# The weight products of a graph layer from three float32r passes over 12-bit parts, with the accumulator kept in DRAM

## The chip, the cores and the metric

The kernel runs on one core of a Trainium2 chip. Times are device microseconds of that core, smaller is better. Abbreviations as in the profile: PE is TensorE (matmuls), PEld its weight loads, DVE is VectorE, ACT is ScalarE, POOL is GpSimd, SP issues DMA transfers. SBUF is the memory on the chip, PSUM holds what the matmuls sum, DRAM is the memory beside it.

## What is computed

Two layers of a graph network on 1250 rows of 1024 columns with 40000 edges, then a mixture of experts, each with a layer normalization ahead of it and added to its input:

```
def _sage_layer(h, edge_src, edge_dst, deg_inv, W_self, W_neigh, b):
    msg = h[edge_src]
    agg = jax.ops.segment_sum(msg, edge_dst, num_segments=h.shape[0])
    mean = agg * deg_inv[:, None]
    return h @ W_self + mean @ W_neigh + b
h   = relu(_sage_layer(layernorm(x), ..., W_self0, W_neigh0, b0))
x   = x + _sage_layer(h, ..., W_self1, W_neigh1, b1)
t   = layernorm(x)
out = x + t + moe(t)       # router rw1, rw2; two of eight experts per row
```

All inputs are fp32. This case is about the second `_sage_layer`: two products of 1250 x 1024 by 1024 x 1024, and one sum over the edges.

## The kernel before

**Stages.** `gnn_windows` turns the edges into a matrix `C` of counts (1250 x 1250) in SBUF while PE does the first layer. The first layer leaves its result transposed in `hT1` (128 partitions, 8 slices k of the 1024 columns, 1250 rows each). Then comes the second layer, and `moe` after it. Rows are worked in 10 blocks of 128 (the last has 98), output columns in two halves of 512.

**Second layer, in order.**
1. `y_half` (L682): y = h times one half of `W_neigh1`, written as two float32r tiles, `zh` (y rounded by ACT) and `zl` (the rest), by `split` (L388).
2. `sum_half` (L697): for each block, 20 float32r matmuls of `C` with `zh` and `zl` (L708), scaled by 1 / degree (`dinv_p`), added to x + b1 (L704 on POOL, L712 on DVE), and stored to `v_d` in DRAM. Both are done for each half.
3. `own_half` (L740): the same kind of product with the two halves of `W_self1`, added to `xa`, a tile of all 10 blocks by 1024 columns that was read back from `v_d` (L734). In the second half each finished block goes to `finish` (L767): `after_layers` (L344) normalizes it (bn_stats L328 and L330, scale L335 on DVE), adds the normalized row (L349 on POOL) and writes both to DRAM, and `turn_back` (L777) transposes it on PE (L784) and copies it with ACT (L788) to `hT1` for the router.

**The products** are plain fp32, by a scheme of seven quarter products instead of eight for a pair of blocks j and 4 + j: `two_blocks` (L630) multiplies the blocks or their sums `T1` to `T4` with the weight quarters or their sums `S1` to `S4` (`weight_sums`, L590; 256 columns a product, L638). DVE makes the sums before a half begins. Blocks 8 and 9 are multiplied directly (`plain_rows`, L621, matmuls L625).

**Memory.** One tile `L` (L91) holds `hT1`, then `SC` (four rows of 1024 columns for scratch and rows) and `WW` (a weight half of 16 KB per partition, which DMA fills: `load_half`, L129). `h0T`, the first layer's input, and later `ts` with the sums share one place (tag "a").

**What sets the order.** A scheduler orders the instructions of each engine before the kernel runs, from the order in the code and its own estimate of when operands are there; each engine then works through its list in that order. `keep_in_program_order` pins the weight loads. In the second layer nothing is ordered by hand. PSUM has rings of three banks `mm` (tile `ps`) and three `mmb` (tile `psb`). The router in `moe` starts with products that need no sums (L1173, L1128), then needs `token_sums` (L1154, DVE, tile `xw`), whose memory is that of the second layer's own tiles, so it waits until the last result row has gone to DRAM.

Of the kernel before, what the change touches and what calls it, by code (L numbers as in the profile page):

```python
# [28 lines left out]
def kernel(  # L29
# [61 lines left out]
    L = land.tile([P, NT + 4 * D + 2 * WQ], F32, name="L")  # L91
    hT1 = L[:, :NT].rearrange("p (k n) -> p k n", k=KD)
    SC = L[:, NT : NT + 4 * D]
    WW = L[:, NT + 4 * D :]

# [32 lines left out]

    def load_half(w, h, t=WW):  # L129

        t = t.rearrange("p (k n) -> p k n", k=KD)
        tc.keep_in_program_order(
            nc.sync.dma_start(
                out=t, in_=w[:, h * HALF : (h + 1) * HALF].rearrange("(k p) n -> p k n", p=P)
            )
        )
        return t
# [206 lines left out]
    def after_layers(b, xa, t):  # L344

        m = rows[b]
        layernorm(t, xa[:, b, :], m)
        nc.sync.dma_start(out=t_d[blk(b), :], in_=t[:m])
        nc.gpsimd.tensor_tensor(xa[:m, b, :], xa[:m, b, :], t[:m], ALU.add)  # L349
        nc.sync.dma_start(out=out[blk(b), :], in_=xa[:m, b, :])  # L350


    def gnn_windows():
# [20 lines left out]
        ones_r = cpool.tile([P, P], F32R, name="ones_r")  # L374
        nc.gpsimd.memset(ones_r.bitcast(F32), 1.0)
# [6 lines left out]
        yl = yp.tile([P, NB, QW], F32R, name="yl")  # L382
        win = yp.tile([P, NB * WIN], F16, name="win")
# [148 lines left out]
        for q in range(4):  # L532
# [8 lines left out]
            if q == 0:  # L541
# [4 lines left out]
                for c0, n in cchunks:  # L546
# [7 lines left out]
                    nc.vector.reciprocal(dinv[:, c0 : c0 + n], dinv[:, c0 : c0 + n])  # L554
            for c0, n in cchunks:
# [23 lines left out]
        NA, KB = 4, KD // 2  # L579
        TC = NA * P  # L580
        ts = apool.tile([P, NB * D], F32, name="ts", tag="a")
        T1, T2, T4 = (
            ts[:, i * KB * TC : (i + 1) * KB * TC].rearrange("p (k n) -> p k n", k=KB)
            for i in range(3)
        )
        B12 = hT1[:, :KB, TC : 2 * TC]
        B22 = hT1[:, KB:, TC : 2 * TC]
        S_first = ts[:, 3 * KB * TC : 3 * KB * TC + 4 * KB * QW]

        def weight_sums(w, s):  # L590
            A11, A12, A21, A22 = w[:, :KB, :QW], w[:, KB:, :QW], w[:, :KB, QW:], w[:, KB:, QW:]
            S1, S2, S3, S4 = (
                s[:, i * KB * QW : (i + 1) * KB * QW].rearrange("p (k n) -> p k n", k=KB)
                for i in range(4)
            )
            tt(S1, A21, A22, ALU.add)
            tt(S2, S1, A11, ALU.subtract)
            tt(S3, A11, A21, ALU.subtract)
            tt(S4, A12, S2, ALU.subtract)
            return A11, A12, A22, S1, S2, S3, S4  # L600

        ws = weight_sums(w_half, S_first)

        tt(T1, B12, hT1[:, :KB, :TC], ALU.subtract)
        for k in range(0, KB, 2):
            ks = slice(k, k + 2)
            tt(T2[:, ks, :], B22[:, ks, :], T1[:, ks, :], ALU.subtract)
            tt(T4[:, ks, :], hT1[:, KB + k : KB + k + 2, :TC], T2[:, ks, :], ALU.subtract)
            for i in (k, k + 1):
                tt(B12[:, i, :], B22[:, i, :], B12[:, i, :], ALU.subtract)  # L610
        T3 = B12

        dinv_p = small.tile([P, NB], F32, name="dinv_p")
        for b in range(NB):
            m = rows[b]
            d_t = tmp[:, b % 4, :P]
            nc.vector.tensor_tensor(d_t[:m, :m], dinv[:m, blk(b)], ident[:m, :m], ALU.mult)  # L617
            nc.vector.tensor_reduce(dinv_p[:m, b : b + 1], d_t[:m, :m], AX.X, ALU.add)
        nc.sync.dma_start(out=row_of(3), in_=bcast(b1, D))

        def plain_rows(w, b):  # L621
            m = rows[b]
            ps = mm.tile([P, 512], F32, name="ps")
            for k in range(KD):
                nc.tensor.matmul(  # L625
                    ps[:m], hT1[:, k, blk(b)], w[:, k, :], start=(k == 0), stop=(k == KD - 1)
                )
            return ps[:m]

        def two_blocks(ws, j, u, store):  # L630

            A11, A12, A22, S1, S2, S3, S4 = ws
            b, b2 = j, NA + j
            js = slice(j * P, (j + 1) * P)

            def product(ps, rows_of, w, first):
                for k in range(KB):
                    nc.tensor.matmul(  # L638
                        ps, rows_of(k), w[:, k, :], start=(first and k == 0),
                        stop=(k == KB - 1), skip_group_check=not first,  # L640
                    )

            u2, u3 = u[:, 0, :], u[:, 1, :]
            pa = mm.tile([P, 512], F32, name="ps")[:, :QW]
            product(pa, lambda k: hT1[:, k, blk(b)], A11, True)
            nc.scalar.copy(u2, pa)
            pb = mm.tile([P, 512], F32, name="ps")[:, :QW]
            product(pb, lambda k: T2[:, k, js], S2, True)
            tt(u2, u2, pb, ALU.add)
            product(pa, lambda k: hT1[:, KB + k, blk(b)], A12, False)  # L650
            store(b, 0, pa, None)
            pc = mmb.tile([P, 512], F32, name="psb")[:, :QW]
            product(pc, lambda k: T3[:, k, js], S3, True)
            tt(u3, u2, pc, ALU.add)
            pd = mmb.tile([P, 512], F32, name="psb")[:, :QW]
            product(pd, lambda k: T1[:, k, js], S1, True)
            store(b2, 1, pd, u3)
            product(pc, lambda k: T4[:, k, js], A22, False)
            store(b, 1, pc, u2)
            product(pd, lambda k: hT1[:, KB + k, blk(b2)], S4, False)  # L660
            store(b2, 0, pd, u2)

        def ring(v, n):
            v = v.rearrange("p (a n) -> p a n", n=QW)
            i = [0]

            def take():
                i[0] += 1
                return v[:, i[0] % n, :]

            return v, take

        us, _ = ring(SC[:, :1024], 4)
        _, spare = ring(SC[:, 1024:2048], 4)
        xs = SC[:, : 3 * D].rearrange("p (a n) -> p a n", n=HALF)
        b1_r = row_of(3)

        with tc.tile_pool(name="y1", bufs=1, side="right") as y1:
# [3 lines left out]
            def y_half(ws):  # L682
                for b in range(2 * NA, NB):
                    split(yh[: rows[b], b, :], yl[: rows[b], b, :], plain_rows(w_half, b))

                def store(b, c, ps, u):
                    if u is not None:
                        t = spare()
                        tt(t, u, ps, ALU.add)
                        ps = t  # L690
                    cs = slice(c * QW, (c + 1) * QW)
                    split(yh[:, b, cs], yl[:, b, cs], ps)
# [38 lines left out]
        for h, order in enumerate((alone + paired, paired + alone)):  # L731
# [3 lines left out]
            if h == 0:  # L735
                w_last = load_half(w_self1, 1, more[:, : 2 * WQ])
# [920 lines left out]
```

## Time and profile before

| What | us |
|---|---|
| Median of 3 runs | 1162.01 (1161.81 to 1162.07) |
| The profiled execution, its own time | 1160.5 |
| Its span from the first to the last instruction | 1158.6 |
| Until the first product of the second layer | 435.75 |
| Second layer, to the router's first product | 349.50 |
| From there to the end | 373.35 |

In the second layer PE is busy for 349.02 of the 349.50 us, DVE for 121.24, POOL for 70.56, ACT for 33.94. A busy time is the sum of the instructions' times on an engine. The time of one matmul overlaps the next, so the rate of PE is read from the distance of starts in the timeline, or from a stretch of time divided by its matmuls.

### The profile page before, as it was taken

The page shows a single profiled execution, that of the slowest core. Times are in us where ns is not written, and L with a number is a line of the kernel's source. Part 1 is how long each engine was busy: PE and PEld are TensorE (multiplying, and loading weights), DVE is VectorE, ACT ScalarE, POOL GpSimd, SP SyncE. Part 2 cuts the span into 40 slices and gives each one's busy share as a digit, 9 for nine tenths or more (in the row PEclk, how much of TensorE's full clock was granted, in tenths as well). Part 3 has the DMA queues.
Part 4 walks back from the last instruction along what each step waited for, and adds up shares of the span by engine and source line. Part 5 has one row for each costly group of instructions (what it writes and reads, how often), then busy time and mean ns, then how long its engine had stood idle before and what let it go on. Part 6 is the DMA issues. An engine that isn't in the chain of part 4 may idle for free.

```text
span 1158.6 us, 13209 instructions
## 1 busy us (share of the span) xinstructions
PE 1122.4 (97%) x4775; PEld 789.3 (68%) x4775; DVE 452.2 (39%) x1127; ACT 181.5 (16%) x420; POOL 331.3 (29%) x438
## 2 busy tenths in 40 slices
PE   6999999999999999999999999999999989999994
PEld 4556556888888886887788688865333666666662
DVE  8767778751212164241234142555221532111110
ACT  5301000001111111100110000122111223222220
POOL 1899999700000000031004011540000013323221
PEclk9999999999999999999999999999999999999997
DMA  7011011010100021042014432347801435554542
GB/s 230 32 40 39 1 37 37 1 37 1 37 1 1 1 73 37 10 170 72 1 34 164 167 118 73 145 164 257 279 19 36 146 89 132 107 121 101 126 116 45
DMA packets 59330, 95.40 MB, mean 82 GB/s; under 512 B 8797, under 2 KB 35645, under 8 KB 59251
## 3 DMA queue, kind: packets, MB, share of 16 engines
q1 hardware_dynamic: 48400, 67.72, 17.0%
q0 software_dynamic: 7056, 23.88, 9.1%
q10 hardware_dynamic: 3798, 2.84, 0.8%
q8 instruction: 42, 0.69, 0.2%
q14 instruction: 34, 0.28, 0.1%
HBM read 68.76 MB, written 27.47 MB: 83 GB/s over the span
## 4 chain that ended last, share of the span: by engine, by line
PE 94%; DVE 2%; ACT 1%; DMA 1%; POOL 1%; issue 0%; ACTq 0%; DVEq 0%; POOLq 0%
PE ps L524 12%; PE ps L458 11%; PE psb L638 9%; PE ps L708 8%; PE ps L560 8%; PE ps L638 7%; PE ps L1493 7%; PE ps L1518 7%; PE ps L1173 5%; PE ps L625 5%; PE ps L1186 4%; PE cnt L419 3%; PE ps L1128 2%; PE tp L1481 2%; PE lg L1105 2%; PE ps L1514 1%
## 5 line engine op out<-in xcount | busy, mean ns | idle before, releaser
L409 POOL TENSOR_SCALAR ol<-lane,keys 125x128 f16<-125x128 f16 x320 | 192.1, 619 | 27.7 <-DVE oh L416 27.7
L458 PE MATMUL ps<-h0T,L 128*128 128x498 f32 (+2 forms) x384 | 147.6, 517 | 0.3 <-ACT h0T L321 0.2
L524 PE MATMUL ps<-L,h0T 128*128 128x256 f32 (+1 forms) x640 | 142.2, 379 | 0.0
L704 POOL TENSOR_TENSOR L<-L 128x512 f32<-128x512 f32 (+1 forms) x20 | 32.0, 1608 | 375.6 <-DVE L L617 217.6
L524 PEld LDWEIGHTS ps<-L,h0T 128*128 128x128 f32 (+1 forms) x640 | 118.3, 187 | 18.0 <-issue 0.6
L416 DVE TENSOR_SCALAR oh<-win,keys 125x240 f16<-125x240 f16 x320 | 85.7, 322 | 30.9 <-PE cnt L419 29.1
L458 PEld LDWEIGHTS ps<-h0T,L 128*128 128x128 f32 x384 | 67.5, 192 | 39.0 <-issue 33.9
L1493 PE MATMUL ps<-xw,L 128*128 x368 | 84.7, 383 | 0.3 <-issue 0.3
L1518 PE MATMUL ps<-xw,L 128*128 x184 | 83.5, 596 | 0.1
L560 PE MATMUL ps<-C,yh 128*128 128x256 f32 (+2 forms) x240 | 81.8, 356 | 0.0
L560 PE MATMUL ps<-C,yl 128*128 128x256 f32 (+2 forms) x240 | 81.5, 353 | 0.0
L708 PE MATMUL ps<-zh,C 128*128 128x512 f32 (+1 forms) x200 | 79.5, 398 | 0.0
L708 PE MATMUL ps<-zl,C 128*128 128x512 f32 (+1 forms) x200 | 78.6, 393 | 0.0
L1493 PEld LDWEIGHTS ps<-xw,L 128*128 128x128 f32 x368 | 69.0, 192 | 10.1 <-issue 1.4
L1529 POOL DMA_INDIRECT out_dram<-L x23 | 36.3, 1579 | 133.4 <-ACT L L1482 87.9
L1470 POOL DMA_INDIRECT L<-t_d,L x26 | 26.0, 1000 | 162.2 <-DVE L L140 142.2
L438 DVE TENSOR_TENSOR C<-C,cnt 128x240 f32 x160 | 64.4, 402 | 13.4 <-DVE oh L416 2.1
L1518 PEld LDWEIGHTS ps<-xw,L 128*128 128x128 f32 x184 | 33.2, 190 | 35.3 <-issue 33.0
L140 DVE TENSOR_TENSOR L<-L,ps 128x512 f32<-128x512 f32 (+1 forms) x28 | 17.1, 611 | 99.7 <-PE ps L1173 47.2
L419 PEld LDWEIGHTS <-ol 125*128 125x128 f16 x320 | 31.0, 97 | 36.6 <-POOL ol L409 21.7
L419 PE MATMUL cnt<-oh,ol 125*128 125x240 f16 x320 | 50.8, 265 | 2.5 <-POOL ol L409 2.1
L1526 DVE TENSOR_SCALAR L<-ps,L 128x512 f32<-128x512 f32 x23 | 17.3, 751 | 91.7 <-PE ps L1518 91.7
(224 smaller groups left out, 1516.6 us busy)
## 6 DMA issues: line engine op xcount, KB each, us to landing
xw<-in_L_ffn_ew_dram SPq DMA_DIRECT2D x16, 1024.0 KB, 7.6
L<-in_x_dram SPq DMA_DIRECT2D x20, 256.0 KB, 2.9
v_d<-L SPq DMA_DIRECT2D x18, 256.0 KB, 2.0
xa<-v_d SPq DMA_DIRECT2D x18, 256.0 KB, 5.9
t_d<-L SPq DMA_DIRECT2D x9, 512.0 KB, 4.4
out_dram<-xa SPq DMA_DIRECT2D x9, 512.0 KB, 4.0
L<-in_L_gnn_W_self_dram SPq DMA_DIRECT2D x4, 1024.0 KB, 5.7
L<-in_L_gnn_W_neigh_dram SPq DMA_DIRECT2D x4, 1024.0 KB
```

The lines of the kernel that those rows point to most:

```text
L409: nc.gpsimd.tensor_scalar(ol[:, c, :], lane[:GP], keys[:, 1, c, r : r + 1], None, op0=ALU.is_equal)
L416: nc.vector.tensor_scalar(oh, win[:GP], keys[:, 0, i * GC + c, r : r + 1], None, op0=ALU.is_equal)
L419: nc.tensor.matmul(ps[:, i, :GW], ol[:, i * GC + c, :], oh, start=(c == 0), stop=(c == GC - 1),)
L438: nc.vector.tensor_tensor(to, to.bitcast(F32), ps[:, i, :GW].rearrange("p (k w) -> p k w", k=NB), ALU.add,)
L458: nc.tensor.matmul(ps[:, :n], w[:, k, (d % 2) * P : (d % 2 + 1) * P], h0T[:, k, c0 : c0 + n], start=(k == 0), stop=(k == KD - 1),)
L524: nc.tensor.matmul(ps[:m, :QW], hT[:, k, blk(b)], w[:, k, :], start=(k == 0), stop=(k == KD - 1))
L560: nc.tensor.matmul(ps[:, :n], part[: rows[k], k, (d % 2) * P : (d % 2 + 1) * P], C[: rows[k], k, c0 : c0 + n], start=(k == 0 and part is y ...
L625: nc.tensor.matmul(ps[:m], hT1[:, k, blk(b)], w[:, k, :], start=(k == 0), stop=(k == KD - 1))
L638: nc.tensor.matmul(ps, rows_of(k), w[:, k, :], start=(first and k == 0), stop=(k == KB - 1), skip_group_check=not first,)
L708: nc.tensor.matmul(ps[:m], C[: rows[k], k, blk(b)], part[: rows[k], k, :], start=(k == 0 and part is yh), stop=(k == NB - 1 and part is yl),)
L1493: nc.tensor.matmul(ps[:, :H], xT[:, k, :], w1_all[:, ds(e, 1), k * H : (k + 1) * H], start=(k == 0), stop=(k == KD - 1),)
L1518: nc.tensor.matmul(ps, hT[:, q, :], w2_all[:, ds(e, 1), q * D + h * HALF : q * D + (h + 1) * HALF], start=False, stop=(q == KH - 1),)
```

## The change

The second layer's products no longer use the seven quarter products. Each operand is cut into three parts, and one product becomes three sums of float32r matmuls, one pass each:

```
def parts_of(a, u, s, l):
    nc.scalar.activation(u, a, AF.Copy, scale=1.0 - B / 2)
    stt(s, u.bitcast(F32), -(1.0 + B), a, op0=ALU.mult, op1=ALU.add)
    nc.gpsimd.tensor_tensor(l, a, u.bitcast(F32), ALU.subtract)
```

with B = 2^-12; u, s and l are float32r. ACT makes u, then DVE makes s and POOL makes l. The products u u, s s and l l are combined with constants:

```
def times(b, w3, pool, t):
    m = rows[b]
    i = n_rows[0] % 2
    n_rows[0] += 1
    sums = [
        (mm, mmb)[i].tile([P, 512], F32, name=("ps", "psb")[i])[:m] for _ in range(3)
    ]
    for k0 in range(0, KD, 2):
        rp = pool.tile([P, 3, 2, P], F32R, name="rp")
        parts_of(hT1[:, k0 : k0 + 2, blk(b)], *(rp[:, j, :, :m] for j in range(3)))
        for j in range(3):
            for k in range(2):
                nc.tensor.matmul(
                    sums[j], rp[:, j, k, :m], w3[:, j, k0 + k, :],
                    start=(k0 + k == 0), stop=(k0 + k == KD - 1),
                )
    nc.scalar.activation(t, sums[0], AF.Copy, scale=1.0 + B)
    stt(t, sums[1], -1.0 / B, t, op0=ALU.mult, op1=ALU.add)
    return sums[2]
```

The weights' parts stand in `wa` (three parts of a half, 48 KB per partition, in the place of `ts`) and `wb` (the last half). `weight_parts` loads two slices k of a weight half (512 KB) and cuts them, four calls a half. The rows' parts `rp` are in rings of three. The calling code, cut to what differs:

```diff
-        ws = weight_sums(w_half, S_first)
-        tt(T1, B12, hT1[:, :KB, :TC], ALU.subtract)
...
+        for k in range(0, KD, 2):
+            ks = slice(k, k + 2)
+            parts_of(w_half[:, ks, :], *(wa[:, j, ks, :] for j in range(3)))
+        first_rows.close()
+        l1a = last_rows.enter_context(tc.tile_pool(name="l1a", bufs=1))
+        l1w = last_rows.enter_context(tc.tile_pool(name="l1w", bufs=2))
+        l1u = last_rows.enter_context(tc.tile_pool(name="l1u", bufs=3))
+        some = l1a.tile([P, 3, HALF], F32, name="some")
+        b1_h = l1a.tile([P, HALF], F32, name="b1_h")
...
+            def y_half():
                 for b in range(NB):
                     m = rows[b]
+                    t = some[:m, b % 2, :]
+                    ll = times(b, wa, l1u, t)
+                    stt(t, ll, 1.0 + 1.0 / B, t, op0=ALU.mult, op1=ALU.add)
+                    nc.scalar.copy(yh[:m, b, :], t)
+                    nc.gpsimd.tensor_tensor(yl[:m, b, :], t, yh[:m, b, :].bitcast(F32), ALU.subtract)
...
-                    v = xs[:m, 5 - b % 6, :]
+                    v = some[:m, 2 - b % 3, :]
                     nc.sync.dma_start(out=v, in_=x[blk(b), hs])
-                    nc.gpsimd.tensor_tensor(v, v, b1_r[:m, hs], ALU.add)
+                    nc.gpsimd.tensor_tensor(v, v, b1_h[:m], ALU.add)
+                    if b in (0, 2, 4, 6):
+                        weight_parts(w_next, h_next, wa, b)
...
-        xa = own.tile([P, NB, D], F32, name="xa")
+        wb = own.tile([P, 3, KD, HALF], F32R, name="wb")
+        own_t = [own.tile([P, HALF], F32, name=f"t{i}") for i in range(2)]
+        own_u = st.enter_context(tc.tile_pool(name="own_u", bufs=3, side="right"))
+        own_v = st.enter_context(tc.tile_pool(name="own_v", bufs=4, side="right"))
...
+        for b in range(NB):
+            v = (some[:m, 2, :], b1_h[:m])[b % 2]
+            nc.sync.dma_start(out=v, in_=v_d[blk(b), :HALF])
+            if b in (0, 2, 4, 6):
+                weight_parts(w_self1, 1, wb, b)
+            t = some[:m, b % 2, :]
+            ll = times(b, wa, l1u, t)
+            nc.gpsimd.tensor_tensor(v, v, t, ALU.add)
+            stt(v, ll, 1.0 + 1.0 / B, v, op0=ALU.mult, op1=ALU.add)
+            nc.sync.dma_start(out=v_d[blk(b), :HALF], in_=v)
...
+        for b in range(NB):
+            v = own_v.tile([P, D], F32, name="v")
+            nc.sync.dma_start(out=v[:m], in_=v_d[blk(b), :])
+            t = own_t[b % 2][:m]
+            ll = times(b, wb, own_u, t)
+            v_h = v[:m, HALF:]
+            nc.gpsimd.tensor_tensor(v_h, v_h, t, ALU.add)
+            stt(v_h, ll, 1.0 + 1.0 / B, v_h, op0=ALU.mult, op1=ALU.add)
+            t = row_of(b)
+            after_layers(b, v, t)
+            turned.append((b, t))
+            if len(turned) > 2:
+                turn_back()
```

So the accumulator of the own products is no longer a whole tile: the first half reads a block of `v_d`, adds and writes it back, the second half reads whole rows into a ring of four. The blocks now come in the order 0 to 9 in every half.

`SC` and `WW` leave `L` for a pool that is closed after the first weight half is cut; `some`, `b1_h`, the weight slices and `rp` take its place until the first own half is over, then it is opened again for the router. b1 is read by halves, x for the sums into three half rows instead of six. `dinv_p` is computed in the first layer's second quarter (q = 1) and no longer after its last, and `ones_r` moves to another pool.

## The prediction on record

> **What bounds the kernel now.** I read the page's busy shares and its chain of work first, then the busy time by stretch of time, then the TensorE (PE) timeline, and last the rows of the operations that the change adds.
>
> ```profile
> PE 1122.4 (97%) x4775; PEld 789.3 (68%) x4775; DVE 452.2 (39%) x1127; ACT 181.5 (16%) x420; POOL 331.3 (29%) x438
> ...
> PE 94%; DVE 2%; ACT 1%; DMA 1%; POOL 1%; issue 0%; ACTq 0%; DVEq 0%; POOLq 0%
> ```
>
> PE carries the chain. That is an average, so I cut out the second graph layer, which runs from 435.75 to 785.25 us. Columns: window, length, busy us of PE, PEld (weight loads), DVE, ACT, POOL, granted clock, DMA share, GB/s.
>
> ```profile
> 435.75:497.65 61.90, 61.90 (x258) 48.08 (x256) 21.22 (x46) 9.21 (x22) 3.79 (x3) 1.00 0.07 23
> 497.65:544.30 46.65, 46.65 (x203) 37.30 (x202) 14.70 (x15) 0.41 (x1) 14.77 (x9) 1.00 0.41 145
> ...
> 652.84:714.92 62.08, 62.08 (x257) 48.24 (x256) 17.96 (x33) 1.49 (x4) 7.97 (x11) 1.00 0.41 138
> 714.92:785.25 70.33, 69.85 (x322) 54.46 (x320) 36.15 (x71) 13.83 (x71) 30.59 (x22) 1.00 0.39 149
> ```
>
> These are the first weight product (a half of 512 columns), the first sum with C, and the two halves of the own product. PE has no idle time in the first three and 0.5 us in the last, at full clock. So a product half costs what its passes through PE cost, and whatever feeds PE is hidden. The change shortens the passes and adds feeders: the question is which is late next.
>
> **The passes.** Timeline of PE (start, us):
>
> ```profile
> 454.67 1.89 PE L638 MATMUL psb<-ts,L 128*128 128x256 f32 x8
> 456.39 1.89 PE L638 MATMUL psb<-ts 128*128 128x256 f32 x8
> ...
> 502.46 0.40 PE L708 MATMUL ps<-zh,C 128*128 128x512 f32 x1
> 502.70 0.40 PE L708 MATMUL ps<-zl,C 128*128 128x512 f32 x1
> ```
>
> A plain fp32 product of four k is 8 instructions, and the next one starts 1.72 us later: 0.215 us per instruction of 256 columns, two per k. A float32r product is one instruction of 512 columns. The 200 of them in the sum stretch take 46.65 us, 0.2333 each. After the change a block is 3 x 8 = 24 such passes, 5.60 us, and a half is 240 x 0.2333 = 56.0 us against 61.9: **5.9 us less per half on PE, 23.6 over four halves**. The sums with C stay.
>
> The Trainium skill ("TensorE: Matmul & The Clock Gate", Back-to-back issue gap) gives N / 2.4 + 2.5 ns at full clock, 216 ns for 512 columns. By it a half would be an estimated 51.8 us and the four halves save 4 x 4.2 us more. The measured 0.2333 stands for the same form, so it decides.
>
> **The feeders.** Groups of instructions in the second layer, shapes kept apart:
>
> ```profile
> L349 POOL TENSOR_TENSOR xa<-xa,L 128x1024 f32<-128x1024 f32 x9 | 21.2, 2353 | 9.2 <-DVE L L335 9.2
> L754 POOL TENSOR_TENSOR xa<-xa,more 128x256 f32<-128x256 f32 x24 | 17.4, 724 | 102.6 <-DVE more L140 94.2 <-DVE rs L334 8.4
> L712 DVE SCALAR_TENSOR_TENSOR L<-ps,dinv_p,L 128x512 f32<-128x512 f32 x18 | 13.5, 749 | 53.3 <-PE ps L708 53.3
> ...
> L390 DVE TENSOR_TENSOR zl<-L,zh 128x256 fp32r<-128x256 f32 x24 | 10.2, 425 | 12.0 <-ACT zh L389 12.0
> L389 ACT CAST zh<-L 128x256 fp32r<-128x256 f32 x24 | 9.7, 404 | 49.5 <-DVE L L140 49.5
> ```
>
> Every block needs four k pairs cut into parts: one ACT (0.40), one DVE (0.42) and one POOL (0.72) instruction of 256 columns each. In a product half POOL adds the low part (512 columns, 1.29), so POOL has 4 x 0.72 + 1.29 = 4.2 us per block, ACT 4 x 0.40 + 2 x 0.59 = 2.8, DVE 4 x 0.42 + 2 x 0.75 = 3.2. All are under 5.60. But DVE and POOL don't run independently (timelines of the two engines during the sums with C, in order of time):
>
> ```profile
> 518.93 1.29 POOL L704 TENSOR_TENSOR L<-L 128x512 f32<-128x512 f32 x1 [2.00 <-DMA L<-in_x_dram]
> ...
> 612.76 1.23 DVE L140 TENSOR_TENSOR ts<-L 128x1024 f32<-128x1024 f32 x1 [0.73 <-DMA L<-in_L_gnn_W_self_dram]
> ...
> 615.20 2.18 POOL L704 TENSOR_TENSOR L<-L 128x512 f32<-128x512 f32 x1
> ...
> 616.15 2.31 DVE L140 TENSOR_TENSOR ts<-ts,L 128x1024 f32<-128x1024 f32 x1
> ...
> 617.34 2.28 POOL L704 TENSOR_TENSOR L<-L 128x512 f32<-128x512 f32 x1
> ...
> 618.39 0.74 DVE L712 SCALAR_TENSOR_TENSOR L<-ps,dinv_p,L 128x512 f32<-128x512 f32 x1
> ```
>
> The same instructions take 1.29 and 1.23 us alone and some 2.2 and 2.3 when they meet: each ends about 1.1 us after the other has ended. They take turns, a DVE one holding 1.07 us for 1024 columns (0.27 for 256), a POOL one 1.15 for 512 (0.58 for 256, 2.22 for 1024), and only some 0.14 us of each lies outside. L712, with one operand in PSUM, ran in its 0.74 beside POOL. So the new cut on DVE, both operands in SBUF, and the cut on POOL take turns: 0.27 + 0.58 = 0.85 us per k pair at least, 1.14 (0.42 + 0.72) if nothing overlaps. I take DVE's hold as three quarters unhidden, 0.20 on top of POOL's 0.72.
>
> The skill says this too ("SBUF — State Buffer", SBUF: two separate sides): the port pair is an exclusive lock held for the whole instruction, and it speaks against the change. By it a k pair would cost the upper 1.14; the rows show the lower end nearer.
>
> **Two product halves (435.75 on).** Turns per block: 4 x 0.85 + 1.15 = 4.6 us at least, 4 x 1.14 + 1.29 = 5.9 at most, around PE's 5.60. The ring of three cuts lets a k pair start two pairs of passes (2.8 us) ahead; its latency is 0.25 + 0.40 + 0.85 = 1.5, so 1.3 us of slack, about what the low part's 1.29 takes once per block. I add 0.14 us per block: 57.4 us, **4.5 less each, -9.0**.
>
> **Sums with C.** Weight cuts (4 x 2.36 on POOL) and x + b1 (10 x 1.29) fit in 46.65 us beside PE: 0. If they didn't, only what exceeds 46 us would show. `dinv_p` is computed earlier, where DVE waits for PE: 0, and up to 6 us of small DVE work if that cover failed. Less x prefetch, the accumulator's round trips and b1 by halves go with SP's transfers: a 256 KB read is 2.9 to 5.9 us, a write 2.0, and the shortest reuse (two own rows) leaves 11.2 us of passes for about 9: 0, and up to 1 us a block if late.
>
> **Entry.** The first weight half is in SBUF at 422.1 (DVE waits for that DMA until then). Its four cuts take turns, 4 x (2.22 + 1.07), with about 2 us of layer-one adds between: 437.4. The first row cut lies on memory that the raw weights held, and needs 1.5 more: PE starts at 438.9 instead of 435.75, **+3** (0 if only the first cut must be over).
>
> **First own half.** Four weight cuts of 2.22 + 1.07 + 0.14 = 3.4 us fall in now, since their target lies where C was. Each overruns the 1.3 us slack by 2.1: 56.0 + 4 x 2.15 = 64.6 against 62.1, **+2.5** (-5 if hidden, +5 if DVE's holds add in full).
>
> **Second own half to the router.** Before, from 714.92 to the first router pass that needs sums of the tokens (802.07) it is 87.15 us: the last residual row is written, lands at 793.14, and 8.9 us of DVE sums follow. After: POOL has per block 2.88 + 1.29 + 2.36 = 6.53 us, and DVE's holds (4 x 0.27 and 0.53 for the normalization, 0.81 us alone) add 1.2: 77.3 for ten. Some 2 us of idle time at its start and 5 in the last row's chain (ACT 0.59, DVE 0.75, POOL 1.29, DVE 0.75, statistics, scale, add) make 84.3. With 3.1 for the write and 8.9: 96.3, **+9.1**. PE needs only 56.0 + 7 for transposes: here POOL and DVE set the end. Downwards -4 (PE alone), upwards +14.
>
> **Sum.** -9.0 + 3 + 2.5 + 9.1 = +5.6 us. The profiled execution took 1160.5 us (span 1158.6 and 1.9 around it), 1.5 below the median 1162.0. So 1166.1 in its terms, **1167.6 us** as a median.
>
> **Rivals.**
> - *The turns are hidden (faster).* If POOL and DVE interleave in each other's fixed times, PE bounds all halves: -11.8 for the two products, -5 for the first own half, -3.5 for the second, +0.5 entry: about -20, 1142 us. For it: 4.6 of 5.60. Against it: 2.2 us where 1.29 is due. Chance 0.24.
> - *The ring is too short (much slower).* Each engine works in a fixed order. If the low part or the accumulator's add stands ahead of the fourth cut on POOL, it takes its 1.29 from a ring that has 1.3, and any DVE hold pushes PE out by 0.8 us a block; over 20 product blocks and the 10 first own blocks that is +24 on PE's 5.60, some +19 on my sum: 1187 us. It decides once a k pair costs more than 1.08 us in turns ((5.60 - 1.29) / 4). For it: the 1.14. Chance 0.22.
> - *It isn't one pass.* If these products took two instructions each as fp32 does, a half would be 112 us and the whole over 1350. The sums' float32r products have one each. Chance 0.02.
>
> **Numbers.** The forecast case has 0.52, its own range 1157 to 1178. The range of 8 in 10, 1144 to 1186, cuts the first rival's lower half and the second's upper half. A measurement tells 0.2% (2.3 us) from no change. Faster: 0.24 and 0.05 of the forecast's lower end, 0.29; within: 0.11; slower: 0.60.
>
> **What would show it.** In the product halves: PE busy with 240 instructions of 0.233 us in 56 to 58 us. POOL's 256-column cuts at 0.9 to 1.0 us in place of 0.72, DVE's at 0.5 to 0.9. In the first own half idle PE of about 2 us near each weight cut; in the second POOL over 80% busy and PE idle for 10 us or more. At the entry PE idle for 3 us. I am wrong if the cuts run at their lone times, if PE is dense in the own halves, or if the passes aren't near 0.233.

## The result, and the profile after

The changed kernel takes 1205.55 us (median of 4 runs, 1204.66 to 1206.02), the kernel before, beside it on the same chip, 1161.91 (4 runs, 1159.98 to 1162.07). The ratio is 1.0379, 95 % interval 1.0361 to 1.0397: 3.8 % slower, 43.6 us. The forecast was 1167.6 with a range to 1186.

The page of the changed kernel, busy shares and chain of work:

```profile
PE 1115.1 (93%) x4711; PEld 778.6 (65%) x4711; DVE 569.4 (47%) x1230; ACT 272.2 (23%) x604; POOL 545.8 (45%) x630
...
PE 79%; POOL 8%; DVE 6%; DMA 2%; issue 2%; ACT 2%; SPq 0%; ACTq 0%; POOLq 0%; DVEq 0%
```

PE's busy time fell by 7.3 us while the span grew by 45.5 (1158.6 to 1204.1): PE now waits. POOL and DVE, which ended 1 % and 2 % of the chain, now end 8 % and 6 %. The second layer cut at the first PE pass of each stage shows where (columns: window, length, busy us of PE, PEld, DVE, ACT, POOL, granted clock, DMA share, GB/s):

```profile
441.61:502.73 61.12, 58.45 (x241) 46.20 (x242) 42.54 (x62) 28.96 (x62) 51.93 (x52) 0.96 0.13 37
502.73:557.94 55.21, 48.83 (x201) 38.44 (x200) 14.79 (x15) 3.04 (x4) 23.78 (x16) 0.94 0.35 116
557.94:616.83 58.89, 56.21 (x242) 44.37 (x240) 41.07 (x60) 28.46 (x60) 49.29 (x49) 1.00 0.06 19
616.83:672.96 56.13, 51.04 (x202) 40.23 (x200) 14.75 (x15) 3.04 (x4) 23.80 (x16) 0.91 0.34 114
672.96:741.52 68.56, 60.54 (x241) 46.58 (x240) 51.33 (x67) 25.84 (x54) 56.09 (x53) 0.93 0.34 117
741.52:846.69 105.17, 84.18 (x373) 58.88 (x372) 78.67 (x111) 37.83 (x142) 69.26 (x58) 1.00 0.47 169
```

In order: product half, sum with C, product half, sum with C, first own half, second own half up to the first router pass that needs the token sums. Where PE's busy time is less than the length it waited; where the clock is below 1.00 it also ran slowly. All kernels in the same cut (us; "entry" is the time from layer one's last pass to the first product pass, less that of the kernel before, where they follow each other without a gap; "rest" is from the end of the second own half's stage to the end of the span):

| Kernel | entry | product | sum | product | sum | own 1 | own 2 | rest | span |
|---|---|---|---|---|---|---|---|---|---|
| before | 0 | 61.90 | 46.65 | 61.90 | 46.64 | 62.08 | 87.15 | 356.5 | 1158.6 |
| forecast, against before | +3 | -4.5 | 0 | -4.5 | 0 | +2.5 | +9.1 | 0 | +5.6 |
| after | 5.95 | 61.12 | 55.21 | 58.89 | 56.13 | 68.56 | 105.17 | 357.4 | 1204.1 |
| after, against before | +5.9 | -0.8 | +8.6 | -3.0 | +9.5 | +6.5 | +18.0 | +0.9 | +45.5 |
| e1, cuts in the sums pinned | 6.50 | 58.09 | 46.84 | 56.75 | 46.87 | 71.34 | 105.25 | 358.2 | 1185.5 |
| e2, rows' low part on DVE | 5.99 | 60.30 | 56.77 | 57.65 | 57.51 | 67.17 | 102.93 | 358.6 | 1203.8 |
| e3, ring of six | 6.16 | 61.15 | 55.20 | 58.89 | 56.12 | 71.77 | 107.14 | 358.5 | 1211.0 |
| e4, without the last add | 6.06 | 62.12 | 55.11 | 58.89 | 54.70 | 68.81 | 86.67 | 357.7 | 1185.7 |
| e5, normalized a block later | 5.92 | 61.03 | 55.17 | 59.16 | 55.91 | 68.18 | 91.59 | 357.2 | 1191.9 |
| e6, cuts in own 1 pinned | 5.94 | 61.07 | 55.01 | 58.97 | 55.91 | 67.04 | 106.74 | 357.4 | 1203.1 |
| e7, sums into the row | 6.36 | 61.17 | 55.24 | 59.09 | 56.03 | 67.30 | 95.38 | 358.0 | 1194.0 |
| e8, e1 + e5 + e6 + e7 | 5.88 | 57.48 | 46.86 | 57.25 | 48.05 | 63.77 | 95.96 | 357.8 | 1168.7 |
| e9, best of each | 6.25 | 58.24 | 47.04 | 57.70 | 46.90 | 64.67 | 91.54 | 359.0 | 1166.6 |
| e10, first cuts pinned | 5.98 | 61.24 | 55.28 | 59.07 | 56.05 | 68.55 | 105.16 | 357.6 | 1205.4 |
| e11, one cut in own 1 | 6.11 | 60.90 | 55.09 | 58.88 | 56.04 | 59.50 | 106.73 | 357.4 | 1199.2 |
| e12, two first cuts | 2.77 | 57.23 | 56.39 | 59.08 | 54.99 | 68.22 | 106.79 | 358.7 | 1199.6 |

Each row is one execution; e9's is the slowest of its five, 3.4 us above their median. A stage that an edit leaves alone still differs from row to row (the second own half between 105.16 and 106.79 in the five kernels that don't change it), and layer one's last pass starts between 434.76 and 438.36 us, so what follows compares stages and not spans.

Three places lose more than the whole 45.5 us: the two sums (+18.1), the second own half (+18.0), and the entry and first own half (+12.4). The product halves give 3.8 back. PE's own rate is as forecast: a dense block of 24 passes takes 5.57 to 5.58 us from start to start, 0.2323 a pass.

**Reading the sums.** The sum's first passes were to find their operands ready. Timeline of POOL in the changed kernel at the end of the first product half (start, us, engine, line, operation, out<-in):

```profile
500.59 1.54 POOL L607 TENSOR_TENSOR rp<-L,rp 128x196 fp32r<-128x196 f32 x1
502.10 2.58 POOL L607 TENSOR_TENSOR wa<-raw,wa 128x1024 fp32r<-128x1024 f32 x1
504.64 3.53 POOL L607 TENSOR_TENSOR rp<-L,rp 128x256 fp32r<-128x256 f32 x3
508.13 1.26 POOL L675 TENSOR_TENSOR some<-some,b_h 128x512 f32<-128x512 f32 x1
509.35 2.34 POOL L607 TENSOR_TENSOR wa<-raw,wa 128x1024 fp32r<-128x1024 f32 x1
511.65 2.24 POOL L665 TENSOR_TENSOR zl<-some,zh 98x512 fp32r<-98x512 f32 x1
```

PE in the same stretch (the bracket is idle time before the instruction and what ended it):

```profile
513.94 0.80 PE L681 MATMUL ps<-zl,C 98*128 98x512 f32 x1 [6.24 <-POOL zl L665]
...
514.96 0.63 PE L681 MATMUL ps<-zl,C 128*128 128x512 f32 x1
515.39 0.63 PE L681 MATMUL ps<-zh,C 128*128 128x512 f32 x1
```

The last low part `zl` (the 98 rows of block 9) is the last operand of the sum's first block. On POOL it stands behind two weight cuts for the next half (`wa`, 2.58 and 2.34 us; one more of 3.43 at 495.85) and behind the next half's first row cuts. PE has nothing to do for 6.24 us. Then its passes start 0.43 us apart instead of 0.23 for eight passes: 1.6 us more. 6.24 + 1.6 is most of this sum's 8.6. In the second sum PE waits 5.09 us in the same place, and 22 slow passes then cost 4.4 us more.

**Reading the second own half.** ACT in two successive blocks of the changed kernel (the bracket is idle time before it and what ended that):

```profile
797.95 0.30 ACT L342 ACTIVATE rs<-mv,eps 128x1 f32<-128x1 f32 x1 [5.34 <-DVE mv L341]
...
807.19 0.29 ACT L342 ACTIVATE rs<-mv,eps 128x1 f32<-128x1 f32 x1 [5.34 <-DVE mv L341]
```

A block takes 9.24 us, though neither POOL (14.58 of 18.50 us busy from 788 on) nor DVE (16.48) is full. ACT stands idle for 5.34 us ahead of the normalization's square root (L342), and the row cuts of the next block stand behind it. DVE and POOL between the two square roots:

```profile
799.20 3.44 DVE L606 SCALAR_TENSOR_TENSOR rp<-rp,L 128x256 fp32r<-128x256 f32 x2
802.57 0.68 DVE L651 SCALAR_TENSOR_TENSOR t<-ps,t 128x512 f32<-128x512 f32 x1
...
803.80 1.46 POOL L740 TENSOR_TENSOR v<-v,t 128x512 f32<-128x512 f32 x1
```

The loop closes: square root at 797.95, two row cuts of the next block on ACT from 798.15, their DVE cuts 799.20 to 802.64 in turn with POOL's add of the row before (L359, 2.57 us), behind them on DVE the block's own sums (L651, though its passes had ended at 799.04), POOL's add L740 to 805.26, DVE's L741, the statistics, and the square root again at 807.19. PE's passes are not on it: they wait for its cuts.

### The profile page after: what moved, and what is told of

The parts are those of the page before. It is cut to its first block, busy times and chain, and to the rows that moved or that the text cites. A ratio compares the mean times of both kernels' runs of the same rounds, so it can differ in the third digit from the quotient of the medians.

```text
span 1204.1 us, 13787 instructions
## 1 busy us (share of the span) xinstructions
PE 1115.1 (93%) x4711; PEld 778.6 (65%) x4711; DVE 569.4 (47%) x1230; ACT 272.2 (23%) x604; POOL 545.8 (45%) x630
## 4 chain that ended last, share of the span: by engine, by line
PE 79%; POOL 8%; DVE 6%; DMA 2%; issue 2%; ACT 2%; SPq 0%; ACTq 0%; POOLq 0%; DVEq 0%
PE ps L534 11%; PE ps L468 10%; PE ps L681 7%; PE ps L646 7%; PE ps L1444 6%; PE ps L1469 6%; PE ps L578 6%; PE psb L646 6%; PE ps L1124 4%; PE ps L1137 4%; PE cnt L429 3%; POOL rp L607 2%; PE ps L1079 2%; PE tp L1432 2%; POOL v L359 2%
## 5 line engine op out<-in xcount | busy, mean ns | idle before, releaser
L607 POOL TENSOR_TENSOR rp<-L,rp 128x256 fp32r<-128x256 f32 (+1 forms) x160 | 137.2, 869 | 51.7 <-ACT rp L605 51.0
L468 PE MATMUL ps<-h0T,WW 128*128 128x498 f32 (+2 forms) x384 | 146.7, 514 | 0.2 <-ACT h0T L331 0.2
L606 DVE SCALAR_TENSOR_TENSOR rp<-rp,L 128x256 fp32r<-128x256 f32 (+1 forms) x160 | 124.7, 790 | 38.2 <-ACT rp L605 35.4
L534 PE MATMUL ps<-WW,h0T 128*128 128x256 f32 (+1 forms) x640 | 142.2, 379 | 0.0
L534 PEld LDWEIGHTS ps<-WW,h0T 128*128 128x128 f32 (+1 forms) x640 | 118.3, 187 | 18.0 <-issue 0.6
L646 PE MATMUL ps<-wa,rp 128*128 128x512 f32 x360 | 91.3, 410 | 10.9 <-ACT rp L605 5.8
L646 PE MATMUL psb<-wa,rp 128*128 128x512 f32 (+1 forms) x360 | 88.9, 401 | 8.3 <-DVE rp L606 4.4
L646 PEld LDWEIGHTS ps<-wa,rp 128*128 128x128 f32 x360 | 70.5, 198 | 29.4 <-DVE rp L606 6.4
L1444 PE MATMUL ps<-xw,L 128*128 x368 | 84.4, 382 | 0.9 <-issue 0.9
L1469 PE MATMUL ps<-xw,SC 128*128 x184 | 83.5, 596 | 0.1
```

Source lines behind the costliest of these rows:

```text
L468: nc.tensor.matmul(ps[:, :n], w[:, k, (d % 2) * P : (d % 2 + 1) * P], h0T[:, k, c0 : c0 + n], start=(k == 0), stop=(k == KD - 1),)
L534: nc.tensor.matmul(ps[:m, :QW], hT[:, k, blk(b)], w[:, k, :], start=(k == 0), stop=(k == KD - 1))
L606: stt(s, u.bitcast(F32), -(1.0 + B), a, op0=ALU.mult, op1=ALU.add)
L607: nc.gpsimd.tensor_tensor(l, a, u.bitcast(F32), ALU.subtract)
L646: nc.tensor.matmul(sums[j], rp[:, j, k, :m], w3[:, j, k0 + k, :], start=(k0 + k == 0), stop=(k0 + k == KD - 1),)
L1444: nc.tensor.matmul(ps[:, :H], xT[:, k, :], w1_all[:, ds(e, 1), k * H : (k + 1) * H], start=(k == 0), stop=(k == KD - 1),)
```

## The experiments

All but e9 are single executions with a profile; the kernel before took 1161.2 to 1162.0 us beside them.

**e1: the weight cuts in the sums keep the place that the code gives them.**

```diff
-            nc.scalar.activation(u, a, AF.Copy, scale=1.0 - B / 2)
+            pin(nc.scalar.activation(u, a, AF.Copy, scale=1.0 - B / 2))
...
-                        weight_parts(w_next, h_next, wa, b)
+                        weight_parts(w_next, h_next, wa, b, tc.keep_in_program_order)
```

> Edit: in the sums with C, ACT's first instruction of each weight cut is kept behind everything that stands ahead of it in the code on ACT, so behind the last block's rounding. Nothing else differs. Stretches of the changed kernel, from the first PE instruction of each to that of the next: product 61.1 and 58.9, sum 55.2 and 56.1, first own half 68.6, second own half to the router's sums 105.2 us. Theory of the order: the cuts of the next weights stand on POOL and DVE ahead of the last block's fourth row cut and low part, and the sum waits for these; then the sums fall to 48 to 50 us, the second product to 56 to 57, and the whole by 14 to 20 us, to about 1188. Theory of the turns (POOL and DVE have too much work that excludes each other, wherever it stands): the cuts only move, what the sums gain is lost behind them, and the whole stays within 4 us of 1205.5.

1187.27 us. The sums fell to 46.84 and 46.87 and the product halves by 3.0 and 2.1. On POOL the last low part now stands ahead of the cuts:

```profile
503.50 1.30 POOL L665 TENSOR_TENSOR zl<-some,zh 98x512 fp32r<-98x512 f32 x1
504.76 4.77 POOL L607 TENSOR_TENSOR wa<-raw,wa 128x1024 fp32r<-128x1024 f32 x2
```

The same eight cuts with the same turns cost the sums nothing in another order: the place in the queue was the cause, not the work. What it did not help is the first own half, which rose to 71.3: there PE now waits 6.54 us in one piece, since two of `wb`'s unpinned cuts stand ahead of the row cuts on DVE (10.05 us from 653.27 on).

**e2: the rows' low part on DVE instead of POOL.**

```diff
-            nc.gpsimd.tensor_tensor(l, a, u.bitcast(F32), ALU.subtract)
+            (low or nc.gpsimd).tensor_tensor(l, a, u.bitcast(F32), ALU.subtract)
...
-                parts_of(hT1[:, k0 : k0 + 2, blk(b)], *(rp[:, j, :, :m] for j in range(3)))
+                parts_of(hT1[:, k0 : k0 + 2, blk(b)], *(rp[:, j, :, :m] for j in range(3)), low=nc.vector)
```

> Edit: the low part of each row cut is made by DVE and not by POOL; the weight cuts stay. Theory of the turns: a row cut now costs DVE 2 x 0.42 us and nobody waits; DVE has 4 x 0.84 + 1.5 + 2.8 = 7.6 us a block in the second own half against 9.26 us a block now, so this half falls from 105 to 85 to 93 us and the whole by 12 to 20; the products stay at 5.58 us a block, since DVE needs 4.9. Rival (the ring of three cuts and the order of the queues set the pace, and turns are small): the row cut is a longer chain on one engine, ACT 0.42, DVE 0.84, and the second own half stays above 103 us or grows. Both leave the sums at 55 to 57 us.

1205.77 us, no change; the second own half gave 2.2 us. DVE was busy for 18.3 of 18.5 us there: one bound gave way to another. The 85 to 93 us of the theory of the turns did not come (102.93), and ACT still waits up to 5.34 us ahead of the square root. The run takes nothing away from the loop and leaves the theories undecided.

**e3: a ring of six row cuts in the second own half, one result row fewer.**

```diff
-        own_u = st.enter_context(tc.tile_pool(name="own_u", bufs=3, side="right"))
-        own_v = st.enter_context(tc.tile_pool(name="own_v", bufs=4, side="right"))
+        own_u = st.enter_context(tc.tile_pool(name="own_u", bufs=6, side="right"))
+        own_v = st.enter_context(tc.tile_pool(name="own_v", bufs=3, side="right"))
```

> Edit: in the second own half the ring of row cuts has six places instead of three, and the ring of accumulator rows three instead of four to make room. Theory of the ring: POOL can cut ahead while it would wait for a place (1.96 us of its 9.26 a block), and the second own half falls from 105 by 10 to 18 us. Theory of the turns: POOL, with 7.3 us of work stretched by waits, takes up most of the 1.96 us at once, and the half falls by 5 us at most. All else equal.

1212.88 us; the half took 107.1 instead of 105.2, and the first own half 71.8. A block in the middle still takes 9.24 us, and ACT still waits 5.90 us ahead of its square root, so the ring's depth is not what holds it. Why the first own half rose is not settled.

**e4: the second own half without POOL's last add (L359).**

```diff
-        nc.gpsimd.tensor_tensor(v[:m], v[:m], t[:m], ALU.add)
+        if add:
+            nc.gpsimd.tensor_tensor(v[:m], v[:m], t[:m], ALU.add)
...
-            after_layers(b, v, t)
+            after_layers(b, v, t, add=False)
```

> Edit: the second own half leaves out the addition of the normalized row to the residual row on POOL (128 x 1024, 2.36 us alone, 2.5 now), so the output lacks that term. If POOL's time sets the pace there, a block falls from 9.26 us to 6.8 to 7.2 and the half from 105 to 78 to 85 us; the whole falls by 20 to 26. If it is DVE or the ring, the half falls by 8 us at most.

1187.46 us; the half took 86.7, 18.5 less. The add's 2.57 us delay the loop by 1.85 a block: it lies on the loop, partly beside DVE's work. That agrees with a loop through POOL and DVE but does not tell what closes it; e5 does.

**e5: each block is normalized one block later.**

```diff
+        def finish():
+            b, v = done.pop(0)
+            t = row_of(b)
+            after_layers(b, v, t, tc.keep_in_program_order)
...
-            t = row_of(b)
-            after_layers(b, v, t)
...
+            done.append((b, v))
+            if b: finish()
+        finish()
```

> Edit: in the second own half the normalization of a block comes after the product of the next block, and its square root on ACT is kept behind ACT's work of that product. Nothing else differs. So far a block takes 9.26 us there, while PE has 6.5 and POOL 7.3 us of work. Theory of the loop: ACT's square root of block b - 1 stands ahead of the row cuts of block b + 1, ACT waits 5.3 us for the statistics on DVE, these wait for the sums on PE, and so the cuts, the passes, the sums and the normalization follow one another in a circle; with the edit the circle is open, the block falls to the turns of POOL and DVE, 7.5 to 8.3 us, and the half from 105 to 88 to 97. Theory of the turns alone: ACT's wait is only a sign of DVE being late, the block stays above 8.9 us and the half above 100.

1193.72 us; the half took 91.6, 13.6 less, with all its work. The same ACT instruction in two successive blocks:

```profile
791.79 0.29 ACT L342 ACTIVATE rs<-mv,eps 128x1 f32<-128x1 f32 x1 [0.52 <-DVE mv L341]
...
799.55 0.30 ACT L342 ACTIVATE rs<-mv,eps 128x1 f32<-128x1 f32 x1 [0.52 <-DVE mv L341]
```

ACT waits 0.52 us where it waited 5.34, and a block takes 7.76 instead of 9.24. DVE is now busy for 15.96 of 16.00 us. The loop made 13.6 of the 18.0 us; what is left is DVE's and POOL's work. The edit moves the whole normalization; that the loop went through ACT's square root is read from this wait, in e8 as well.

**e6: the weight cuts in the first own half pinned**, as in e1, at `weight_parts(w_self1, 1, wb, b, tc.keep_in_program_order)`.

> Edit: in the first own half ACT's first instruction of each weight cut is kept behind everything that stands ahead of it in the code on ACT, so that the four cuts are spread over the blocks 0, 2, 4 and 6. So far two stand at the beginning and two in the second block, and the half takes 68.6 us. Theory of the order: each cut costs what exceeds the ring's slack, about 2 us, and the half falls to 63 to 66. Theory of the turns: the cuts cost the same 12 us wherever they stand, and the half stays at 67 to 70.

1204.93 us; the half took 67.0, 1.5 less. The cuts were spread over blocks 0, 2, 4 and 6, but PE still waited for DVE cuts near them (2.19, 2.40 and 2.20 us in the third, fifth and seventh block). PE's idle time in the half even rose, from 8.02 to 9.13 us; what the spreading saved is slow clock (1.00 in place of 0.93), as no single wait is long now. Here their place is not the main cost.

**e7: DVE adds the three sums straight into the row**, without ACT's scaling into `t` and POOL's add, in both own halves.

```diff
+            if add:
+                stt(t, sums[0], 1.0 + B, t, op0=ALU.mult, op1=ALU.add)
...
-            ll = times(b, wa, l1u, t)
-            nc.gpsimd.tensor_tensor(v, v, t, ALU.add)
+            ll = times(b, wa, l1u, v, True)
```

> Edit: in both own halves DVE adds the three sums straight to the accumulator (three instructions with one operand in PSUM, 0.7 us each), in place of ACT's scaling, DVE's two and POOL's 1.29 us addition. Theory of the loop: the circle in the second own half loses ACT 0.6, POOL 1.3 to 1.45 and gains 0.7, so a block falls from 9.26 to 7.8 to 8.4 us and the half from 105 to 90 to 97. Theory of the turns: POOL has 1.3 us less per block that excludes DVE, about the same fall in both halves, 68.6 to 63 to 66 in the first as well. If DVE, with 0.7 us more, is the bound, neither falls by more than 3 us. This run alone doesn't tell loop from turns; it does together with the run that normalizes later.

1195.80 us: own halves 67.3 and 95.4. The second is what the theory of the loop had (90 to 97), the first is above the 63 to 66 of the theory of the turns. The edit shortens the loop by POOL's add but leaves it closed: ACT still waits 2.10 to 5.17 us ahead of L342 in the middle blocks.

**e8: e1, e5, e6 and e7 together.**

> All of the edits: weight cuts kept in the order of the code in the sums and in the first own half, normalization one block later, sums straight into the accumulator. If each takes away what the theories of order and loop say, the products take 58 and 57 us, the sums 47 each, the first own half 60 to 63, the second 82 to 88 up to the router's sums, entry and rest as before: 1148 to 1160 us for the whole, just under the 1162 of the kernel before. By the theory of the turns the own halves stay at 66 and 97 or more, and the whole stays above 1172.

1170.55 us. The first own half is at 63.8, below each of its parts alone, but the second is at 96.0, worse than e5. ACT waits 5.16 us ahead of L342 again: the loop is closed. My reading is that the pin holds the square root behind the last ACT instruction of a block, which is a row cut once ACT's scaling is gone. e9, which keeps the scaling and POOL's add in this half and is otherwise the same kernel, waits 0.52 us there and takes 91.5; that agrees, but no run moves the pin alone.

**e11: three of the four weight cuts left out of the first own half.**

```diff
-            if b in (0, 2, 4, 6):
+            if b == 0:
                 weight_parts(w_self1, 1, wb, b)
...
-                            sums[j], rp[:, j, k, :m], w3[:, j, k0 + k, :],
+                            sums[j], rp[:, j, k, :m], w3[:, j, (0 if one else k0) + k, :],
```

> Leaves out three of the four weight cuts in the first own half; the second own half then reads the one cut pair for all four (its products are not the reference's, the passes are as many). If the 6.5 us that this half is longer than before come from the weight cuts on GpSimd and VectorE between the row cuts, three quarters of them go: the half takes 62 to 64 us in place of 68.6, the total 1199 to 1201 us, all other stages unchanged. If they come from the rows' own work (four row cuts and an add on GpSimd, some 5 us per block, in turn with VectorE), the half stays at 66 to 68 us.

1201.23 us; the half took 59.50, 9.06 less, 3.0 us per cut. With all four gone, if the fourth costs as much, it would be 68.56 - 4 x 3.02 = 56.5, PE's own 56. So the cuts are the half's whole excess over dense passes. Of the 9.06 us, 5.6 are idle time of PE (8.02 us in the changed kernel, 2.42 here), the rest is mostly slow clock (0.93 there, 1.00 here). In the changed kernel POOL's timeline at this half's start has two of them in a row:

```profile
674.34 6.73 POOL L607 TENSOR_TENSOR wb<-raw,wb 128x1024 fp32r<-128x1024 f32 x2 [8.54 <-ACT wb L605]
```

and PE's timeline the wait that follows, and the next one:

```profile
681.41 1.76 PE L646 MATMUL ps<-wa,rp 128*128 128x512 f32 x4 [3.63 <-DVE rp L606]
...
691.77 1.81 PE L646 MATMUL psb<-wa,rp 128*128 128x512 f32 x4 [2.93 <-DVE rp L606]
```

**e10: the last two first cuts pinned behind layer one.**

```diff
-            parts_of(w_half[:, ks, :], *(wa[:, j, ks, :] for j in range(3)))
+            parts_of(
+                w_half[:, ks, :], *(wa[:, j, ks, :] for j in range(3)),
+                *([tc.keep_in_program_order] if k >= 4 else []),
+            )
```

> Only the last two of the four first weight cuts are put behind layer one's last ScalarE instruction. If the entry of 5.9 us comes from the weight cuts that stand between layer one's last adds on VectorE (2.83 to 3.42 us each), the first product pass comes 2 to 3 us earlier (entry 3 to 4 us), and the first product half takes back about as much, because block 0 then waits for the last two cuts: the total stays within 2 us of the changed kernel. If the entry comes from the latency of the first row cut instead (u, then s and l, about 2.5 us) and the adds only follow their own waits, the entry stays at 5 to 6 us and the total rises by the 3 to 5 us of the late cuts.

1207.19 us, entry 5.98. The pin moved nothing: ACT still made all four cuts at once at 422.91, and DVE's cuts stood between layer one's adds as before. It tells nothing; e12 takes the work away instead.

**e12: the last two first cuts left out.**

```diff
-        for k in range(0, KD, 2):
+        for k in (0, 2):
...
-                            sums[j], rp[:, j, k, :m], w3[:, j, k0 + k, :],
+                            sums[j], rp[:, j, k, :m], w3[:, j, k0 % pairs + k, :],
...
-            y_half()
+            y_half(4)
             sum_half(0, w_neigh1, 1)
```

> Leaves out the last two of the four first weight cuts; the first product half reads the two cut pairs in place of all four (its products are not the reference's, the passes are as many). If the entry of 5.9 us comes from the cuts that stand between layer one's last adds on VectorE (the last two of them take 3.42 and 2.83 us), those adds end 3 to 6 us earlier, as soon as the last layer-one passes let them, and the first product pass comes 2.5 to 4 us after layer one's last pass: entry 2.5 to 4 us, the total 1201.5 to 1203.5 us, all other stages unchanged. If the entry is the chain of the last two adds, the ReLU and the first row cut by itself, which no weight cut lengthens, it stays at 5.5 us or above and the total at 1204 to 1206 us.

1201.63 us, entry 2.77. Timeline of DVE in the changed kernel around layer one's last passes (last start 435.43; 435.23 in e12):

```profile
430.48 3.42 DVE L606 SCALAR_TENSOR_TENSOR wa<-wa,WW 128x1024 fp32r<-128x1024 f32 x1
...
434.40 2.83 DVE L606 SCALAR_TENSOR_TENSOR wa<-wa,WW 128x1024 fp32r<-128x1024 f32 x1
...
439.73 0.68 DVE L586 TENSOR_TENSOR SC<-SC,L 128x496 f32<-128x496 f32 x1
```

The last of these adds in e12's timeline of DVE:

```profile
436.36 0.68 DVE L586 TENSOR_TENSOR SC<-SC,L 128x496 f32<-128x496 f32 x1
```

Without the two cuts layer one's last add starts 3.4 us earlier (3.2 counted from the last pass), and the first row cut, which stands behind the last ReLU on ACT, with it. So 3.2 of the entry's 5.95 us are theirs. The other 2.8 are the chain that stays: the last two adds from 435.65 on, the ReLU at 437.07, the row cut at 437.77, the first pass at 438.23. The product half fell too (57.23): the next cuts happened to fall behind block 9's row cuts there, as e1 forces, so that part is not the entry's.

**e9: e1, e5 and e6, with e7's edit in the first own half alone.**

> Three cures together, each where a run alone showed it to work: the cuts of the next weight half stand in the queues behind what the code has ahead of them (in both sums and in the first own half), the first own half adds its three sums directly into the row on VectorE, and the second own half normalizes each block one block later, with its three sums still taken over ScalarE and GpSimd. If the three causes are separate (queue order in the sums, GpSimd's weight cuts in the first own half, the loop through the square root in the second), the stages are the best of the single runs: products 57.5 and 57, sums 47 and 47, own halves 64 and 92, entry 6, the rest 358, together 1164 to 1167 us, within 0.5 % of the kernel before. If they hold each other up (the freed time is taken back by VectorE and GpSimd in turn), the time stays at 1170 or above.

Median 1165.17 us of 5 runs (1164.77 to 1168.53) against 1161.17 of 8: ratio 1.0035, interval 1.0021 to 1.0050. The sums, products and second own half are within 1.0 us of the best single run with all of its work and the first own half is below any, so the causes can be cured separately. Of the 43.6 us lost, 39.6 are back, all but some 2.4 of them (the direct sums in the first own half, 64.67 against e6's 67.04) by order alone. The scheme so ordered is still 4.0 us slower than the kernel before.

## Why the prediction was wrong, point by point

**Passes: right.** 0.2333 us were forecast and 0.2323 measured. "It isn't one pass" is out.

**Product halves: the term was right, its neighbourhood wrong.** 57.4 us each were forecast, 61.12 and 58.89 came. With e1's order they are 58.09 and 56.75, 57.4 on average, but that this meets the forecast is luck. The 57.4 were 56.0 of passes and 1.4 of small waits; in e1 the first half has no wait at all (PE busy for 58.09 of 58.09 us), and the 2.3 us above 240 x 0.2323 = 55.8 are passes at half clock after the entry. The second has one wait of 0.74 us. Turns do lengthen the cuts, and the passes hide them. Groups of the changed kernel in the second layer (after the bars: busy us and mean ns of one, then idle us ahead and what ended it):

```profile
L607 POOL TENSOR_TENSOR rp<-L,rp 128x256 fp32r<-128x256 f32 x144 | 124.4, 875 | 46.6 <-ACT rp L605 46.5
L606 DVE SCALAR_TENSOR_TENSOR rp<-rp,L 128x256 fp32r<-128x256 f32 x144 | 110.4, 778 | 35.3 <-ACT rp L605 32.7
```

724 ns became 875 on POOL and 425 became 778 on DVE. In the product halves alone, for which the 0.9 to 1.0 and the 0.5 to 0.9 were given, they are 894 to 899 and 605 to 621, just below the one and within the other.

**Sums with C: the step that failed.** "Weight cuts (4 x 2.36 on POOL) and x + b1 (10 x 1.29) fit in 46.65 us beside PE: 0. If they didn't, only what exceeds 46 us would show." They fit: POOL was busy for 23.8 us of each sum. But I added up a stage's work and left out its order. The target of the first cut is free as soon as block 9's first passes are over, the scheduler put it there, and on an engine that works in order it delays what PE needs next. It cost 17.6 of the sums' 18.1 us and 5.2 in the product halves (e1; 18.6 in the span, after its dearer first own half). I also had no term for the half clock after a long wait: 1.6 and 4.4 us of the two sums.

**Second own half: right work, missed loop.** I had 7.73 us a block from POOL's and DVE's turns; with the loop opened (e5) a block in the middle takes 7.76. The closeness is partly luck: my sum had POOL full, e5 has DVE full and POOL at 14.62 of 16.00 us, and the half as a whole takes 91.6 and not my 96.3. I placed the excess on occupancy and did not follow the wait through the square root to the next block's row cuts: 13.6 us. My "up to +14" did not reach the +18.0.

**First own half: the waits were right, the clock was left out.** 2.15 us of waiting per weight cut were forecast; PE's idle time is 8.02 us, 2.0 per cut, and 2.2 to 2.4 near three of the cuts where they are spread (e6). But two cuts came in a row, the waits grew to 3.63 and 2.93 us, and 18 passes at half clock cost 3.7 us more. With them a cut costs 3.0 (e11).

**Entry: mis-sized.** I had the cuts over at 437.4 and "about 2 us of layer-one adds between". The cuts were over at 436.2 on POOL and 437.2 on DVE, as forecast, but five of layer one's small DVE instructions came behind them, up to 440.4, and the first row cut behind the last ReLU. Beyond +5.9 the idle time halves the clock: the first block of passes took 7.81 us from start to start instead of 5.58.

**The rivals.** "The ring is too short" named the right kind of cause, an instruction ahead of the one PE needs, in the wrong place: product blocks ran dense, and a ring of six gave nothing (e3). "The turns are hidden" is right in its outcome for the product halves alone. Neither held the loop, nor cuts of the next stage ahead of the last operand of this one.

## What to carry to other kernels

Work that "fits beside PE" costs nothing only if it stands in its queue behind what PE needs next: at a stage's end, ask which instruction of the next stage can start early, and what then waits behind it. Where a block's last step on an engine stands ahead of the next block's first, add up the chain from one to the other; it bounds the block even if no engine is full, and doing that last step one block later opens it. Test such an order by pinning it, but look in the trace whether the pin moved anything.

## What the runs showed of the hardware

**Waiting costs PE twice.** After 6.24 us of idle time in the first sum the granted clock was 0.50 for the next 4.1 us (passes 0.43 us apart), and 0.50 for 4.0 us after the 5.79 us at the entry; the waits of 0.3 to 1.7 us between the second own half's products left it at 1.00. The Trainium skill ("TensorE: Matmul & The Clock Gate", Part 1: The HAM clock gate) says that an idle window of about 3.4 us halves the clock until a busy window has passed, and gives 426.7 ns for 512 columns then. The passes 0.43 us apart and the two long waits agree. But a shorter wait is enough: after the 2.93 us in the first own half the clock is 0.50 for 6.8 us (columns as above):

```profile
692.20:698.80 6.60, 5.14 (x13) 3.54 (x12) 5.92 (x5) 0.83 (x2) 6.60 (x6) 0.50 0.35 119
```

The clock records of these traces change only at steps of 3.41 us, in the changed kernel at 681.86, 685.27, 692.10 and 698.92 among others. Counted over all 14 traces between 400 and 860 us, every such step at full clock in which PE was idle for over 1.83 us was followed by half clock, and none with less than 1.61 us of idle time was. So about half of a step is enough; the page's 3.4 us of idle time are not needed. e9's wait of 2.63 us, of which no step held more than 1.53, left the clock at 1.00.

**A cut on two engines is dear to both.** Alone an instruction of 256 columns took 0.72 us on POOL and 0.42 on DVE; as cuts beside each other they averaged 0.875 and 0.778, a sum of 1.65 for what is 1.14 one after the other. The time of each holds its wait for the other: in the second own half two DVE cuts that take 0.41 alone spread over 3.44 us beside POOL's add of 2.57. So the busy shares of the two can't be added, and a full DVE (15.96 of 16.00 us in e5) is partly a waiting one.
